# A scan kernel with experts: half a quad more of the products with C on GpSimdE, the last states copied there, and two groups of experts' products per slot

## The chip, the cores and the metric

One core of a Trainium2 chip runs the whole program. Time is device time of one launch in microseconds; the number that counts is the median of the runs shown. The profile is of one further execution, with its own time.

In the profile PE is TensorE's matmul, PEld its weight load, DVE is VectorE, ACT is ScalarE, POOL is GpSimdE, SP is SyncE, which here issues most DMAs.

## The reference, cut to what matters

The input x has 2 batches of 256 channels and 4096 positions (64 x 64). All is fp32.

```
# layer 0: group norm, then one selective scan with 256 inner channels
x = x + scan_block(gn(x), L0)
# layer 1, tokens t: norm, two selective scans with 512 inner channels, forward (f) and backward (b)
t = tokens(x)
xn = ln(ln(t)) * gamma + beta
t = t + scan_block(xn, f) + flip(scan_block(flip(xn), b)) + ln(t)
# experts: 8 of them, all used, weighted by a softmax over the mean of the batches
h = relu(bn(ln(t) @ W1[e] + b1)); h = relu(bn(h @ W2[e] + b2)); y = h @ Wo[e] + bo
t = t + sum_e w[e] * y[e]

def scan_block(x):
    xs, z = split(x @ W_in); xc = silu(conv4(xs)); dt, B, C = split(xc @ W_x); dt = softplus(dt @ W_dt + b)
    for each position:                                   # 16 states n for each inner channel d
        h[d, n] = h[d, n] * exp(dt[d] * A[d, n]) + dt[d] * xc[d] * B[n]
        y[d] = sum_n h[d, n] * C[n] + D[d] * xc[d]
    return (y * silu(z)) @ W_out
```

## The kernel before

**Stages.** After a short start (group norm of batch 0) come the scans: six jobs in this order, layer 0, f, b of batch 0, then of batch 1. A job runs over 8 chunks of 512 positions. Then comes the experts' stage, for what is left of the 8 experts on 8 chunks of 2 batches (128 units).

**Quads and passes.** 128 inner channels times 16 states are laid on the partitions so that one tile of 128 x 4 x 512 (a quad, tile `bq`) holds four groups of 32 channels by four states. Eight quads (two blocks j of 128 channels, four groups of states sg each) are a pass. Layer 0 has one pass per chunk, f and b have two: 80 passes, 640 quads. A quad is scanned in two halves of 128 x 1024; a half quad is a slot, the unit of the hand-written order, 16 to a pass.

**One quad's way.** POOL multiplies dt*x by B into `bq` (`emit_b`, L652, 128x2048), three quads ahead of the scan. ACT computes the decay exp(dt*A) of a half into a PSUM tile `da` (`emit_decay`, L662; two buffers) and joins the state carried from the chunk before (L673). DVE scans the half (`emit_scan`, L683). Then the product with C: for quads 0, 2 and 5 of a pass (`POOL_C`, L61) the scan writes back into `bq` and POOL multiplies the whole quad (`emit_times_c_quad`, L708); for the five others the scan writes into `da`, and DVE multiplies each half out of `da` into `bq` (`emit_times_c`, L692). PE sums over the states (`emit_sum`, L713, 128*32 weights `stack`) into `y`; DVE gates y (L732). The last state of each quad goes into `h_state` for the next chunk (`emit_carry`): ACT copies it from `da` (L702, two columns per half) or from `bq` (L704, four columns per quad), and for the POOL quads the product may overwrite `bq` only after that copy.

**Order.** Every engine works in the order in which the program issues to it; the loop at L1002 writes this order out, slot by slot. Within a slot: SP's loads, PE's work (`pe`, the sums, `pe2`), ACT's carry and next decay and `act`, then DVE: queue `dve0`, the scan, queue `dve`, the product with C; then POOL by the table `POOL_AT` (L64; "c0" is the product of quad 0, "b3" the B product three quads on), and queue `pool`. The `Slots` object holds work placed at a slot and queue.

**Work beside the scans.** While a chunk is scanned, the next one is prepared (`prepare`): in-projection xs and z (L412), convolution (L450), x-projection (L479), dt (L499), softplus, the gate z: PE at a slot, ACT's tanh (L537) one slot later, DVE's L541 into `sz` two slots later in queue `dve0`, ahead of that slot's scan. For f and b the slots of dt and z lie in the second pass of the chunk before, as do POOL's products xdt (L515) and f's norm (`norm`, L377 to L398: DVE divides, POOL adds, ACT applies the affine map at L385, one slot after the division). When b has finished a chunk, its features are normalised (`features`) and the experts can begin on it.

**The experts' planner** (`experts`, L837 to L894) fills PE's spare time in the scans. It walks the slots and keeps sums of what each slot already holds (`sl.count`: products, ACT operations, PSUM banks with the slots for which they are held). PE may take `PE_ROOM` 3.8 products a slot and be `PE_BEHIND` 2.5 behind; ACT likewise. One expert on one chunk of one batch is three layers (W1, W2, Wo) of two groups m of two matmuls; `follows` says the earliest slot of a layer's next group. At most one group is put into a slot. The units so placed are written to DRAM; 67 of the 128 are done before the scans end, the eight chunks of batch 0 and 3 experts of chunk 7 of batch 1.

**The experts' stage** (from L1050) does the 61 left: for each, W1 and W2 on PE (L1189) with ACT's relu (L1193), weights on DVE (L1200), Wo on PE (L1208). Chunks with something left are in `rest`, those complete in both batches in `whole` (none before). Side work is placed between: the routing of the next chunk (`routes`), the bias and the weighted sums of units done early (`sums`; L1159 and L1160 on DVE).

Of the kernel before, what the change touches and what calls it, by code (L numbers as in the profile page):

```python
# [44 lines left out]
ALU = mybir.AluOpType  # L45
AX = mybir.AxisListType

P = 128
NB, C, L = 2, 256, 4096
KC = C // P  # L50
# [9 lines left out]

POOL_C = (0, 2, 5)  # L61

SUMS = {(0, 0): (-1,), (2, 0): (0, 1), (4, 0): (2, 3), (5, 1): (4,), (7, 0): (5, 6)}
POOL_AT = {0: "b3", 1: "c0 b4", 2: "b5", 3: "c2 b6", 4: "b7", 5: "b8", 6: "c5 b9", 7: "b10"}  # L64
HUGE = 1e37


# [62 lines left out]
def hybrid_kernel(ctx: ExitStack, tc: tile.TileContext, a: dict, out: bass.AP):  # L130
# [53 lines left out]
    with ExitStack() as st:  # L184
# [129 lines left out]
        def norm(i):  # L314
# [79 lines left out]
            for d, queue, fn in (  # L394
                (-48, "sp", load_x), (-44, "pe", mean), (-43, "dve", centre), (-42, "act", square),
                (-41, "pe", variance), (-40, "act", roots), (-39, "dve", divide), (-39, "pool", add),
                (-38, "act", affine), (-36, "sp", store),
            ):  # L398

                sl.put(s0 + d + (6 if c == 0 else 0), queue, fn)  # L400
# [2 lines left out]
            sl.count(s0 - 43, 0, 1)  # L403
            sl.count(s0 - 41, 2, 4, (2,))
            sl.count(s0 - 40, 0, 0, (1,))
            sl.count(s0 - 39, 0, 2)

        def in_proj(job, ck, half, j, name):
            ps = psp.tile([P, T], F32, tag="ps", name=name)
# [8 lines left out]
        def prepare(i):  # L418
# [109 lines left out]
            def gate(j):  # L528

                v = {}  # L530

                def pe():
                    v["ps"] = in_proj(job, ck, 1, j, f"z_{tag}_{j}")

                def act():
                    v["th"] = wk.tile([P, T], F32, tag="th", name=f"thz_{tag}_{j}", bufs=3)
                    nc.scalar.activation(v["th"], v["ps"], AF.Tanh, scale=0.5)  # L537

                def dve():
                    ck["sz", j] = wk.tile([P, T], F32, tag="sz", name=f"sz_{tag}_{j}", bufs=8)  # L540
                    nc.vector.scalar_tensor_tensor(  # L541
                        ck["sz", j], v["th"], 1.0, v["ps"], ALU.add, ALU.mult
                    )

                return (0, "pe", pe), (1, "act", act), (2, "dve0", dve)

            def put(slot, work):
                for d, queue, fn in work:
# [5 lines left out]
            for j in range(nj):  # L554
                put(at["xs"][j], xs(j))
                sl.count(s0 + at["xs"][j], 2, 1, (1,))
                put(at["dt"][j], softplus(j))
                sl.count(s0 + at["dt"][j], 1, 3, (2,))
                sl.count(s0 + at["z"][j], 2, 1, (1,))
            for jp in range(nj // 2):  # L560
                put(at["conv"][jp], conv(jp))
                sl.count(s0 + at["conv"][jp], 5, 1, (1, 2))
# [82 lines left out]
        def over_groups(t):  # L645
            return t.rearrange("p (o t) -> p o t", o=1).to_broadcast([P, SG, T])
# [20 lines left out]
        def emit_join(g, h):  # L667
# [4 lines left out]
            if c:  # L672
# [2 lines left out]
                    scale=cks[i]["a0", j][:, h, sg : sg + 1], bias=bq[g][:, q, 0:1],  # L675
                )

        def emit_scan(g, h):
            i, j, sg = at(g)
            job, c = steps[i]  # L680
            d = da[g, h].rearrange("p q t -> p (q t)")
            b = bq[g][:, 2 * h : 2 * h + 2, :].rearrange("p q t -> p (q t)")
            nc.vector.tensor_tensor_scan(  # L683
                b if quads[g][2] in POOL_C else d, d, b,
                job.h[:, j, sg, 2 * h : 2 * h + 1] if c else 0.0, ALU.mult, ALU.add,
            )

# [9 lines left out]
        def emit_carry(g, h):  # L697

            i, j, sg = at(g)
            d, two = da.pop((g, h)), slice(2 * h, 2 * h + 2)  # L700
            if quads[g][2] not in POOL_C:
                nc.scalar.copy(steps[i][0].h[:, j, sg, two], d[:, :, T - 1])  # L702
            elif h:
                nc.scalar.copy(steps[i][0].h[:, j, sg, :], bq[g][:, :, T - 1])  # L704

        def emit_times_c_quad(g):
            i, j, sg = at(g)
            nc.gpsimd.tensor_tensor(bq[g], bq[g], over_groups(cks[i]["bc", 1, sg]), ALU.mult)  # L708

        def emit_sum(g):  # L710
            i, j, sg = at(g)
# [125 lines left out]
        def experts():  # L837
# [4 lines left out]
            def fits(slot):  # L842

                at = sum(b[0] <= slot for b in banks)
                both = banks[:at] + [(slot, slot + 1, 0)] + banks[at:]
                return all(
                    both[k - 3][1] + both[k][2] <= both[k][0] for k in range(max(3, at - 2), min(len(both), at + 4))
                    if at in range(k - 3, k + 1)
                )
# [9 lines left out]
            def follows(l):  # L859

                k, m = divmod(len(times[l]), KC)
                if k == len(todo):
                    return None
                waits = [(l - 1, k * KC + 1, 2)] if l else []
                if m:
                    waits.append((l, k * KC, 1))
                elif k:

                    waits.append((l, k * KC - 1, 6 if l == 0 and todo[k][-1] == 0 else 5))
                    if l < 2:  # L870
                        waits.append((l + 1, k * KC - 1, 0))
                if any(n >= len(times[w]) for w, n, _ in waits):
                    return None
                return max([todo[k][0] + 3] + [times[w][n] + d for w, n, d in waits])

            for slot in range(last):
                behind = max(0.0, behind) + sl.products.get(slot, 0) + sums_in(slot) - PE_ROOM
                act_behind = max(0.0, act_behind) + sl.acts.get(slot + 1, 0) - ACT_ROOM
                if behind + 2 > PE_BEHIND or act_behind + 1.3 > ACT_BEHIND or not fits(slot):
                    continue  # L880
                for l in (2, 1, 0):
                    at = follows(l)
                    if at is None or slot < at:
                        continue
                    banks.insert(sum(b[0] <= slot for b in banks), (slot, slot + 1, 0))
                    times[l].append(slot)
                    behind += 2
                    act_behind += 1 if l == 2 else 1.3
                    break
            put = [  # L890
                (*item[1:], [times[l][k * KC + m] for l in range(3) for m in range(KC)])
                for k, item in enumerate(todo) if (k + 1) * KC <= len(times[2])
# [109 lines left out]
        for g in range(nq):  # L1002
            i, jp, n = quads[g]
            for h in range(2):
# [24 lines left out]
                sl.run(slot, "dve0")  # L1029
                emit_scan(g, h)  # L1030
                sl.run(slot, "dve")
                if n not in POOL_C:
                    emit_times_c(g, h)

                if h == 0:
                    for what in POOL_AT.get(n, "").split():
                        m = g - n + int(what[1:])
                        if what[0] == "c":
                            emit_times_c_quad(m)
                        else:  # L1040
                            want_b(m)
                sl.run(slot, "pool")
# [7 lines left out]
    with ExitStack() as st:  # L1050
# [171 lines left out]
        side = {i: [] for i in rest}  # L1222
        for at, i in enumerate(rest):
            after = rest[at + 1 : at + 2]
            now = sums(i)
            if at:
                for j in whole[at - 1 : at]:
                    now += sums(j)
            ahead = []
            for j in whole[at : at + 1] + after:  # L1230
                ahead += routes(j)
            every = max(1, len(now) // max(1, len(ahead)))
            work = side[i]
            while now or ahead:
                work += ahead[:1] + now[:every]
                ahead, now = ahead[1:], now[every:]
# [143 lines left out]
```

## Time and profile before

| what | us |
|---|---|
| median of 3 runs | 5331.44 (5330.82 to 5335.3) |
| the profiled execution | 5329.55 |
| its span | 5327.7 |
| DVE busy in it | 4647.7 |
| PE busy in it | 4401.2 |
| POOL busy in it | 4271.5 |
| ACT busy in it | 3707.4 |
| first scan starts | 61.1 |
| last scan starts | 4588.9 |

The busy times are over the whole span, which mixes the two stages; the page's row of 40 slices shows DVE and POOL full for the first 34 of them and PE full in the last five. A row of a group reads: line, engine, operation, output from inputs, shape, count, then busy time and the mean of one. A row of waits reads: who waited for whom, total us, times, longest.

### The profile page before, as it was taken

What the parts mean: (1) busy time and instruction counts of PE and PEld (TensorE: products, weight loads), DVE (VectorE), ACT (ScalarE), POOL (GpSimd) and SP (SyncE); (2) the same over time, 40 slices, a digit from 0 to 9 for tenths busy, and PEclk for the clock granted to TensorE, in tenths of its full rate; (3) what the DMA queues carried; (4) which work ended last, traced back from release to release, by engine and by line L of the source; (5) the groups of instructions that cost most, each with busy time, mean ns of one, the idle gap of its engine ahead of it and who ended that gap; (6) DMA issues with size and microseconds to landing.
All of it is one profiled execution on the core that took longest, in us unless ns stands there. A gap on an engine that the chain in (4) does not pass through costs nothing.

```text
span 5327.7 us, 47305 instructions
## 1 busy us (share of the span) xinstructions
PE 4401.2 (83%) x14920; PEld 1499.7 (28%) x14920; DVE 4647.7 (87%) x3117; ACT 3707.4 (70%) x7728; POOL 4271.5 (80%) x1118
## 2 busy tenths in 40 slices
PE   5677767766678898888878888888998988699999
PEld 1122222221122233222222232233332332244444
DVE  6999999999999999999989999999999999554333
ACT  5677676776767777878887777788778877422332
POOL 6898999999998999998989999999999999411010
PEclk8778788888889999999999999899999999899999
DMA  4445433344334554455555444454545444332332
GB/s 172 139 173 180 139 124 134 127 152 147 131 129 156 189 177 160 164 175 181 191 192 178 160 157 155 166 186 163 178 149 184 171 167 159 132 138 103 111 103 75
DMA packets 306860, 821.11 MB, mean 154 GB/s; under 512 B 34664, under 2 KB 96112, under 8 KB 264624
## 3 DMA queue, kind: packets, MB, share of 16 engines
q1 hardware_dynamic: 302896, 792.78, 43.5%
q0 software_dynamic: 3712, 25.30, 1.2%
q8 instruction: 118, 1.93, 0.1%
q14 instruction: 134, 1.10, 0.1%
HBM read 637.48 MB, written 180.49 MB: 154 GB/s over the span
## 4 chain that ended last, share of the span: by engine, by line
DVE 42%; PE 26%; ACT 12%; issue 9%; POOL 5%; DMA 3%; SPq 0%; DVEq 0%; POOLq 0%; ACTq 0%
DVE da L683 21%; DVE bq L692 8%; PE hp L1189 8%; DVE bq L683 8%; ACT da L662 5%; PE y L1208 4%; PE e L903 3%; POOL bq L652 3%; PE y L713 2%; PE conv L450 2%; PE xs L412 2%; PE o L751 2%; DMA rdt<-dtd 1%; DVE sz L541 1%; PE dbc L479 1%
## 5 line engine op out<-in xcount | busy, mean ns | idle before, releaser
L652 POOL TENSOR_TENSOR bq<-rxdt,bc 128x2048 f32<-128x2048 f32 x640 | 2891.9, 4542 | 42.6 <-issue 20.5
L662 ACT ACTIVATE da<-rdt,w_a 128x512 f32<-128x512 f32 x2560 | 1756.4, 686 | 90.2 <-DVE bq L683 43.9
L683 DVE TENSOR_TENSOR_SCAN da<-da,h_state,bq 128x1024 f32<-128x1024 f32 x700 | 1643.9, 2348 | 12.7 <-issue 8.0
L708 POOL TENSOR_TENSOR bq<-bq,bc 128x2048 f32<-128x2048 f32 x240 | 1086.5, 4527 | 300.9 <-ACT h_state L704 279.8
L713 PE MATMUL y<-bq,stack 128*32 128x512 f32 x5120 | 849.7, 678 | 340.0 <-POOL bq L708 207.1
L692 DVE TENSOR_TENSOR bq<-da,bc 128x1024 f32<-128x1024 f32 x800 | 978.4, 1223 | 24.0
L683 DVE TENSOR_TENSOR_SCAN bq<-da,h_state,bq 128x1024 f32<-128x1024 f32 x420 | 965.1, 2334 | 24.2 <-ACT da L662 24.2
L702 ACT COPY h_state<-da 128x2 f32<-128x2 f32 x799 | 125.8, 157 | 794.0 <-DVE bq L692 792.7
L903 PE MATMUL e<-eh,ew 128*128 128x512 f32 x1072 | 539.6, 631 | 55.4 <-ACT eh L914 27.5
L1193 ACT ACTIVATE h<-hp,of,sc 128x512 f32<-128x512 f32 x244 | 189.6, 777 | 391.6 <-PE hp L1189 375.0
L673 ACT ACTIVATE bq<-h_state,bq,a 128x1 f32<-128x1 f32 x1120 | 431.9, 386 | 0.0
L713 PEld LDWEIGHTS y<-bq,stack 128*32 128x32 f32 x5120 | 152.3, 117 | 984.9 <-issue 376.8
L412 PE MATMUL z<-nx,w_in 128*128 128x512 f32 x640 | 337.9, 656 | 69.5 <-DVE sp L511 46.8
L412 PE MATMUL xs<-nx,w_in 128*128 128x512 f32 x640 | 338.2, 663 | 39.4 <-DVE xc L464 30.3
L450 PE MATMUL conv<-xs,w_conv 64*64 64x512 f32 x2560 | 329.6, 623 | 6.5 <-DVE sp L511 3.6
L903 PEld LDWEIGHTS e<-eh,ew 128*128 128x128 f32 x1072 | 196.2, 197 | 398.4 <-issue 231.8
L751 PE MATMUL o<-sz,w_out 128*128 128x512 f32 x640 | 299.7, 608 | 0.0
L903 PE MATMUL e<-en,ew 128*128 128x512 f32 x536 | 261.3, 614 | 26.5 <-DVE fcen L799 13.3
L1200 DVE TENSOR_TENSOR h<-h,wb 128x1024 f32<-128x1024 f32 x61 | 74.3, 1221 | 210.5 <-ACT h L1193 192.4
L1132 POOL DMA_DIRECT2D w_dram<-wts x8 | 4.3, 544 | 315.3 <-ACT wts L1130 315.3
L720 PE MATMUL y<-xc,w_d 128*128 128x512 f32 x320 | 186.6, 667 | 71.3 <-DVE sz L732 71.3
L515 POOL TENSOR_TENSOR xdt<-sp,xc 128x512 f32<-128x512 f32 x160 | 203.2, 1274 | 44.3 <-DVE sp L511 44.3
(138 smaller groups left out, 5446.2 us busy)
## 6 DMA issues: line engine op xcount, KB each, us to landing
rxdt<-xdtd SPq DMA_DIRECT2D x160, 1024.0 KB, 6.3
rdt<-dtd SPq DMA_DIRECT2D x160, 1024.0 KB, 5.9
bc<-bcd SPq DMA_DIRECT2D x384, 256.0 KB, 3.1
dtd<-sp SPq DMA_DIRECT2D x160, 256.0 KB, 3.6
xdtd<-xdt SPq DMA_DIRECT2D x160, 256.0 KB, 2.8
ew<-in_W SPq DMA_DIRECT2D x134, 256.0 KB, 4.1
u<-eu SPq DMA_DIRECT2D x67, 512.0 KB, 3.9
u<-u SPq DMA_DIRECT2D x67, 512.0 KB, 3.6
```

The costliest lines, as they stand in the source:

```text
L412: nc.tensor.matmul(ps, job.w["in", half][:, k, j * P : (j + 1) * P], rhs, start=(k == 0), stop=(k == KC - 1),)
L450: nc.tensor.matmul(v[r][64 * col : 64 * col + 64, :], job.w["conv"][rows, 2 * jp + j, k, :], ck["xs", jp][rows, j, k : k + T] if k < 4 els ...
L652: nc.gpsimd.tensor_tensor(bq[g], ck["rxdt", j], over_groups(ck["bc", 0, sg]), ALU.mult)
L662: nc.scalar.activation(da[g, h][:, k, :], cks[i]["rdt", j][:, q, :], AF.Exp, scale=steps[i][0].w["a"][:, j, q * SG + sg : q * SG + sg + 1],)
L673: nc.scalar.activation(bq[g][:, q, 0:1], job.h[:, j, sg, q : q + 1], AF.Identity, scale=cks[i]["a0", j][:, h, sg : sg + 1], bias=bq[g][:, ...
L683: nc.vector.tensor_tensor_scan(b if quads[g][2] in POOL_C else d, d, b, job.h[:, j, sg, 2 * h : 2 * h + 1] if c else 0.0, ALU.mult, ALU.add,)
L692: nc.vector.tensor_tensor(bq[g][:, two, :], d, cks[i]["bc", 1, sg].rearrange("p (o t) -> p o t", o=1).to_broadcast([P, 2, T]), ALU.mult,)
L708: nc.gpsimd.tensor_tensor(bq[g], bq[g], over_groups(cks[i]["bc", 1, sg]), ALU.mult)
L713: nc.tensor.matmul(y[i, j][q * CG : (q + 1) * CG, :], stack, bq[g][:, q, :], start=False, stop=(sg == SG - 1),)
L751: nc.tensor.matmul(v[m], job.w["out"][:, j, m * P : (m + 1) * P], ck["sz", j], start=False, stop=(j == job.nj - 1),)
L903: nc.tensor.matmul(ps, ew[l][:, k, m * P : (m + 1) * P], key[x][:, k, :], start=(k == 0), stop=(k == KC - 1),)
L1189: nc.tensor.matmul(ps, we[f"W{l + 1}", e][:, k, m * P : (m + 1) * P], x[:, k, :], start=(k == 0), stop=(k == KC - 1),)
```

## The change

1. In every second pass (`g // QN % 2`; for f and b the second pass of a chunk) the first half of quad 4 joins the POOL quads: its scan writes into `bq` and POOL multiplies 128x1024 by C (`h4` ahead of `b8`).
2. POOL copies the last states of all its quads itself, just before the product ("tensor_copy" ahead of "tensor_tensor"), in place of ACT.
3. The gate's DVE operation moves from queue `dve0` to `dve`, that is from ahead of the scan to behind it, and the planner counts its bank for two slots. The norm's affine map moves one slot later (except in a job's first chunk).
4. The planner may put more than one group into a slot, both groups of a layer into the same one, and the planner's count of the norm's affine moves by one slot.
5. In the experts' stage the sums of a complete chunk come first in a chunk's side work, and no longer between the routings.

```diff
--- before.py
+++ after.py
@@ -60,8 +60,10 @@
 
 POOL_C = (0, 2, 5)
 
+POOL_HALF = (4, 0)
+
 SUMS = {(0, 0): (-1,), (2, 0): (0, 1), (4, 0): (2, 3), (5, 1): (4,), (7, 0): (5, 6)}
-POOL_AT = {0: "b3", 1: "c0 b4", 2: "b5", 3: "c2 b6", 4: "b7", 5: "b8", 6: "c5 b9", 7: "b10"}
+POOL_AT = {0: "b3", 1: "c0 b4", 2: "b5", 3: "c2 b6", 4: "b7", 5: "h4 b8", 6: "c5 b9", 7: "b10"}
 HUGE = 1e37
 
 
@@ -394,7 +396,7 @@
             for d, queue, fn in (
                 (-48, "sp", load_x), (-44, "pe", mean), (-43, "dve", centre), (-42, "act", square),
                 (-41, "pe", variance), (-40, "act", roots), (-39, "dve", divide), (-39, "pool", add),
-                (-38, "act", affine), (-36, "sp", store),
+                (-37 if c else -38, "act", affine), (-36, "sp", store),
             ):
 
                 sl.put(s0 + d + (6 if c == 0 else 0), queue, fn)
@@ -403,7 +405,7 @@
             sl.count(s0 - 43, 0, 1)
             sl.count(s0 - 41, 2, 4, (2,))
             sl.count(s0 - 40, 0, 0, (1,))
-            sl.count(s0 - 39, 0, 2)
+            sl.count(s0 - 38, 0, 2)
 
         def in_proj(job, ck, half, j, name):
             ps = psp.tile([P, T], F32, tag="ps", name=name)
@@ -542,7 +544,7 @@
                         ck["sz", j], v["th"], 1.0, v["ps"], ALU.add, ALU.mult
                     )
 
-                return (0, "pe", pe), (1, "act", act), (2, "dve0", dve)
+                return (0, "pe", pe), (1, "act", act), (2, "dve", dve)
 
             def put(slot, work):
                 for d, queue, fn in work:
@@ -556,7 +558,7 @@
                 sl.count(s0 + at["xs"][j], 2, 1, (1,))
                 put(at["dt"][j], softplus(j))
                 sl.count(s0 + at["dt"][j], 1, 3, (2,))
-                sl.count(s0 + at["z"][j], 2, 1, (1,))
+                sl.count(s0 + at["z"][j], 2, 1, (2,))
             for jp in range(nj // 2):
                 put(at["conv"][jp], conv(jp))
                 sl.count(s0 + at["conv"][jp], 5, 1, (1, 2))
@@ -675,13 +677,18 @@
                     scale=cks[i]["a0", j][:, h, sg : sg + 1], bias=bq[g][:, q, 0:1],
                 )
 
+        def on_pool(g, h):
+
+            n = quads[g][2]
+            return n in POOL_C or (n, h) == POOL_HALF and g // QN % 2
+
         def emit_scan(g, h):
             i, j, sg = at(g)
             job, c = steps[i]
             d = da[g, h].rearrange("p q t -> p (q t)")
             b = bq[g][:, 2 * h : 2 * h + 2, :].rearrange("p q t -> p (q t)")
             nc.vector.tensor_tensor_scan(
-                b if quads[g][2] in POOL_C else d, d, b,
+                b if on_pool(g, h) else d, d, b,
                 job.h[:, j, sg, 2 * h : 2 * h + 1] if c else 0.0, ALU.mult, ALU.add,
             )
 
@@ -698,14 +705,17 @@
 
             i, j, sg = at(g)
             d, two = da.pop((g, h)), slice(2 * h, 2 * h + 2)
-            if quads[g][2] not in POOL_C:
+            if not on_pool(g, h):
                 nc.scalar.copy(steps[i][0].h[:, j, sg, two], d[:, :, T - 1])
-            elif h:
-                nc.scalar.copy(steps[i][0].h[:, j, sg, :], bq[g][:, :, T - 1])
-
-        def emit_times_c_quad(g):
+
+        def emit_times_c_quad(g, groups=SG):
             i, j, sg = at(g)
-            nc.gpsimd.tensor_tensor(bq[g], bq[g], over_groups(cks[i]["bc", 1, sg]), ALU.mult)
+            b = bq[g][:, :groups, :]
+            nc.gpsimd.tensor_copy(steps[i][0].h[:, j, sg, :groups], b[:, :, T - 1])
+            nc.gpsimd.tensor_tensor(
+                b, b,
+                cks[i]["bc", 1, sg].rearrange("p (o t) -> p o t", o=1).to_broadcast([P, groups, T]), ALU.mult,
+            )
 
         def emit_sum(g):
             i, j, sg = at(g)
@@ -863,7 +873,7 @@
                     return None
                 waits = [(l - 1, k * KC + 1, 2)] if l else []
                 if m:
-                    waits.append((l, k * KC, 1))
+                    waits.append((l, k * KC, 0))
                 elif k:
 
                     waits.append((l, k * KC - 1, 6 if l == 0 and todo[k][-1] == 0 else 5))
@@ -876,17 +886,16 @@
             for slot in range(last):
                 behind = max(0.0, behind) + sl.products.get(slot, 0) + sums_in(slot) - PE_ROOM
                 act_behind = max(0.0, act_behind) + sl.acts.get(slot + 1, 0) - ACT_ROOM
-                if behind + 2 > PE_BEHIND or act_behind + 1.3 > ACT_BEHIND or not fits(slot):
-                    continue
-                for l in (2, 1, 0):
+                for l in (2, 1, 1, 0, 0):
                     at = follows(l)
                     if at is None or slot < at:
                         continue
+                    if behind + 2 > PE_BEHIND or act_behind + 1.3 > ACT_BEHIND or not fits(slot):
+                        break
                     banks.insert(sum(b[0] <= slot for b in banks), (slot, slot + 1, 0))
                     times[l].append(slot)
                     behind += 2
                     act_behind += 1 if l == 2 else 1.3
-                    break
             put = [
                 (*item[1:], [times[l][k * KC + m] for l in range(3) for m in range(KC)])
                 for k, item in enumerate(todo) if (k + 1) * KC <= len(times[2])
@@ -1029,7 +1038,7 @@
                 sl.run(slot, "dve0")
                 emit_scan(g, h)
                 sl.run(slot, "dve")
-                if n not in POOL_C:
+                if not on_pool(g, h):
                     emit_times_c(g, h)
 
                 if h == 0:
@@ -1037,6 +1046,9 @@
                         m = g - n + int(what[1:])
                         if what[0] == "c":
                             emit_times_c_quad(m)
+                        elif what[0] == "h":
+                            if on_pool(m, 0):
+                                emit_times_c_quad(m, SG // 2)
                         else:
                             want_b(m)
                 sl.run(slot, "pool")
@@ -1222,15 +1234,14 @@
         side = {i: [] for i in rest}
         for at, i in enumerate(rest):
             after = rest[at + 1 : at + 2]
-            now = sums(i)
+            now, work = sums(i), side[i]
             if at:
                 for j in whole[at - 1 : at]:
-                    now += sums(j)
+                    work += sums(j)
             ahead = []
             for j in whole[at : at + 1] + after:
                 ahead += routes(j)
             every = max(1, len(now) // max(1, len(ahead)))
-            work = side[i]
             while now or ahead:
                 work += ahead[:1] + now[:every]
                 ahead, now = ahead[1:], now[every:]
```

## The prediction

> **What bounds the kernel now.** I read the page first, then a table of busy time by stretch, then who waits for whom, then the order of time. The kernel has two stages. The scans (the 80 passes of 16 half quads) fill 61.07 to 4592.4 us; the six stretches below are the jobs (layer 0, f, b of each batch) and the seventh is the experts' stage, 735.3 us.
>
> ```profile
> core 0: us, PE busy (x) PEld busy (x) DVE busy (x) ACT busy (x) POOL busy (x), PEclk, DMA share, GB/s
> 61.07:540.70 479.63, 335.61 (x1166) 97.05 (x1168) 453.02 (x287) 352.81 (x746) 432.94 (x111) 0.80 0.48 163
> 540.70:1438.80 898.10, 632.35 (x2316) 184.19 (x2312) 868.21 (x565) 642.03 (x1398) 839.49 (x214) 0.85 0.40 137
> 1438.80:2341.20 902.40, 756.68 (x2712) 250.21 (x2708) 872.62 (x578) 689.04 (x1474) 831.73 (x208) 0.92 0.47 160
> 2341.20:2815.20 474.00, 398.98 (x1418) 129.59 (x1420) 438.21 (x286) 390.22 (x807) 423.37 (x109) 0.96 0.57 191
> 2815.20:3716.30 901.10, 781.39 (x2794) 263.83 (x2792) 868.88 (x564) 711.86 (x1518) 842.55 (x215) 0.93 0.49 166
> 3716.30:4592.40 876.10, 763.63 (x2716) 260.26 (x2712) 857.13 (x547) 686.55 (x1459) 812.68 (x201) 0.95 0.47 158
> 4592.40:5327.70 735.30, 701.14 (x1688) 302.16 (x1688) 271.95 (x255) 211.27 (x283) 79.88 (x56) 0.98 0.33 115
> ```
>
> In the scans DVE is busy 4358 of 4531 us (96%), POOL 4183 (92%). So DVE bounds this stage and POOL stands 175 us behind it: work that leaves DVE for POOL is worth only what POOL can take. In the experts' stage PE is busy 95%.
>
> Inside a chunk the two passes differ. Here are passes 52 and 53 (job f) and 72 and 73 (job b):
>
> ```profile
> 3040.70:3093.00 52.30, 49.58 (x210) 16.89 (x207) 51.96 (x34) 39.83 (x89) 48.44 (x12) 1.00 0.43 144
> 3093.00:3154.40 61.40, 47.86 (x141) 16.03 (x141) 57.66 (x40) 50.03 (x104) 57.72 (x17) 0.86 0.54 189
> 4156.40:4208.70 52.30, 51.03 (x214) 17.54 (x211) 51.95 (x34) 40.82 (x91) 48.87 (x12) 1.00 0.35 121
> 4208.70:4267.30 58.60, 49.67 (x151) 16.39 (x150) 56.55 (x40) 48.38 (x102) 55.41 (x16) 0.91 0.60 202
> ```
>
> The second pass of a chunk is the long one, and in job f DVE stands still 3.7 us of it. The waits say why:
>
> ```profile
> DVE sz L541 <- ACT thz L537: 66.3, 39, 4.1
> DVE xc L464 <- ACT thx L459: 34.6, 14, 15.3
> DVE bq L683 <- ACT da L662: 28.1, 24, 2.2
> POOL bq L708 <- ACT h_state L704: 279.8, 113, 7.2
> ```
>
> The gate's L541 stands ahead of the scan and waits for ACT's tanh: 66 us. Most of POOL's rest is the product with C (L708) waiting until ACT has copied the last states.
>
> **What the Trainium skill says.** "GPSIMD Engine Reference", 3.1 "Elementwise — side-by-side cycle accounting", gives 4497 ns for a two-input operation of 2048 columns. The trace agrees: 4542 and 4527 ns, starts 4.48 us apart. The same page, 1 "Specifications", says the SBUF interfaces are shared with VectorE, contended by DVE instructions with two SBUF inputs; L683 and L692 take one input from PSUM, and no run here shows such a collision. "Perfetto Trace Analysis", "GPSIMD Engine Instruction", advises timing by spacing of starts, which I do. "TensorE: Matmul & The Clock Gate", Part 1, says idleness throttles PE: granted clock rises here from 0.80 to 0.96 as PE's busy share in the jobs rises from 0.70 to 0.84, so products that fill gaps partly pay for themselves.
>
> **The change part by part.**
>
> 1. *Half quad 4 in every second pass.* 40 passes, one L692 each. Spacing of starts gives what a half quad costs DVE:
>
> ```profile
> 3049.31 2.35 DVE L683 TENSOR_TENSOR_SCAN da<-da,h_state,bq 128x1024 f32<-128x1024 f32 x1
> 3051.70 1.23 DVE L692 TENSOR_TENSOR bq<-da,bc 128x1024 f32<-128x1024 f32 x1
> 3052.84 4.58 DVE L683 TENSOR_TENSOR_SCAN bq<-da,h_state,bq 128x1024 f32<-128x1024 f32 x2
> 3057.34 2.33 DVE L683 TENSOR_TENSOR_SCAN da<-da,h_state,bq 128x1024 f32<-128x1024 f32 x1
> ```
>
> With product 3052.84 - 3049.31 = 3.53 us; without, (3057.34 - 3052.84)/2 = 2.25. So DVE loses 1.28 x 40 = 51 us. POOL gains 40 products of 128x1024 at 2.30 us (spacing behind L381, same shape: 3018.18 to 3020.48), 92 us.
>
> 2. *POOL copies last states.* 240 + 40 = 280 copies of 4 or 2 columns, and each product waits for POOL's own copy. The trace shows none. Below: spacings of 1.23 us for 512 columns and 4.48 for 2048 leave 0.15 us at no columns. Above: nothing so small is near 1 us; POOL's setup rows of 128x128 take 0.20 and 0.29 us; I bound it at 0.7 us, four times the lower, for the wait on its own result. A gain is not excluded: the link over ACT goes (in a waiting case, scan end 3045.29, ACT's copy to 3045.53, product 3045.60), about 0.2 us in the 113 waiting products. I take 0.3 us each: 84 us. Queued behind a waiting copy are its product and the B products of quads three ahead; DVE's scans need them only six half quads later, PE's sums at once. ACT loses 240 copies of 190 ns and 40 of 157 (52 us); ACT is busy 77% of the scans, so this costs and gives nothing by itself.
>
> 3. *Gate behind the scan* (dve0 to dve). L541 gets 2.3 us more; the mean wait was 66.3/39 = 1.7 us, the longest 4.1. Alone worth some 50 to 60 us, if nothing else is late next. The later affine (one slot) relieves ACT, which waited 16 us for POOL's L381. Its price is a PSUM bank held a slot longer; the planner counts it.
>
> What is late next is POOL, so I add up a pair of passes (one chunk of f or b, two of layer 0), means over the jobs:
> - f: 112.4 us now, DVE 108.6, POOL 105.1. After: DVE 107.3, POOL 105.1 + 2.3 + 7 x 0.3 = 109.5. POOL is now the fuller; with 1 us of waits 110.5. Gain 1.9 x 16 = 30 us.
> - b: 111.2 now, DVE 108.1, POOL 102.8. After: DVE 106.8, POOL 107.2; with 2 us of waits (3 now) 109.1. Gain 2.1 x 16 = 34.
> - layer 0: 119.2 now, after 1.3 less for the product and 1.2 for the gate (9.9 us of that wait lie in its 8 pairs). Gain 2.5 x 8 = 20.
> Together 84 us.
>
> 4. *Two products in one slot.* Counted in the program's order: 888 expert matmuls before the end of the scans instead of 804, so 74 experts instead of 67; 54 are left. In the last stage one expert takes PE
>
> ```profile
> 5252.04 4.29 PE hp L1189 x10
> 5256.33 0.01 issue
> 5256.34 2.84 PE hp L1189 x6
> 5259.19 3.43 PE y L1208 x8
> 5262.62 4.29 PE hp L1189 x10
> ```
>
> 10.58 us, on the chain that ends the program. 7 x 10.58 = 74 us less. Chunk 7 is then complete in both batches; its routing and its 16 weighted sums stay in the stage, beside PE (DVE 37% busy there; 7 more sums at 1.32 + 1.40 = 2.7 us are 19 us). Changed order of that side work: nothing, hidden by the same idle DVE; uncovered, at most the 16 us standstill at the stage's start (4642.74, "issue", on the chain) could grow or vanish, so 74 +- 10. In the scans PE takes on 84 matmuls at (539.6 + 261.3)/804 = 1.0 us, 84 us or 1.6 per pass over 53 passes, and SP 28 more DMAs (21 weights, 7 stores) that wait in order behind PE. The fullest even passes of b already carry 18 matmuls at 52.3 us, as long as those with 14, and the new order gives 18 nearly everywhere. Not free everywhere: from 0 to 40 us through later y, conv and z; I take 15. The new short slots want the decay sooner: 28.1 us over 240 such quads is 0.12 each; 40 x 0.12 = 5.
>
> Sum: scans -84 + 15 + 5 = -64, experts' stage -74, together -138. The profiled execution took 5329.6 us, its span 5327.7 and 1.9 around it: 5329.6 - 138 = 5191.6. The median of the runs is 1.9 higher: 5193.5, and I say 5193.
>
> **The rivals.**
> - *POOL becomes the bound outright.* A copy with its wait costs 0.7 us: f needs 105.1 + 2.3 + 4.9 = 112.3, all of today's 112.4; b 110.0 plus 1 of wait, nothing; layer 0 keeps some 10. Scans -10, stage -74: 5247. For it: the profile has no row for the copy, and pass 53 already fills POOL 57.7 of 61.4 us. Against: spacing leaves little fixed cost.
> - *DVE gets everything.* POOL's lag in the second pass is made good in the first (48.4 of 52.3), the lead of three quads (21 us) hides it, and the ACT link's removal pays for the copies. DVE's 51 + 55 of the gate, less 10: scans -96, stage -76: 5159. For it: the lead; against: f's sum of 109.5 allows only -46 in f.
> - *Slower.* One mechanism, the copy on POOL (L708's place, before each product). With 92 + 280c on top of 4183 and about 60 us of waits, POOL fills 4531 + 74 us, that is eats the gain of the experts' stage, at c = 0.97 us. At c = 1.3 the scans take 4699, 168 more, less 74: 5425.
> - *PE too full.* The two products in a slot delay y and z by more than my 15, 60 us: 5238. For it: PE 50 of 52 us busy in first passes; against: the rising clock.
> That the change doesn't do what it says is excluded by the order of the program: 40 halves, 280 copies and 74 experts stand in it.
>
> **How the numbers follow.** Forecast 0.60 (its own range 5170 to 5222: stage +-10, copies 0.15 to 0.5 us, PE 0 to 30), POOL outright 0.12, DVE everything 0.15, PE too full 0.07, slower 0.06. The range leaves out the slower case and the far halves of the others: 5152 to 5245. 0.2% is 11 us, about what a measurement of this kernel tells from no change. Faster by more: 0.92; within: 0.02 (the far end of PE too full); slower: 0.06.
>
> **What would show it right or wrong.** Stage after the last scan: near 661 us, 54 x 24 products. Scans: about 4467 us. POOL's copies: spacing to their product near 0.3 us. L541's wait for thz: under 20 us. Pairs of f: near 110.5 with POOL over 98% busy and L708's wait small; if DVE is instead the fuller, the second rival holds. POOL busy over 99% with DVE waiting for L652 shows the first. I am wrong if the copies cost over 0.7 us, or if DVE's waits for y (L732), thx or thz grow by over 40 us.

## The result and the profile after

The changed kernel takes 5211.78 us (median of 4 runs, 5208.79 to 5213.06), the kernel before 5332.59 us beside it: ratio 0.9773, 95% interval 0.976 to 0.9787. That is 121 us less; 138 were forecast, and the range from 5170 to 5222 us holds. The profiled execution took 5213.1 us, its span is 5211.3.

The same cut of the span as before, behind the last scan and its product: start, end and length of the stretch, busy us (instructions) of each engine, granted clock, DMA share, GB/s. First the kernel after, then the one before, cut in two likewise.

```profile
60.71:4529.40 4468.69, 3633.04 (x13280) 1201.78 (x13280) 4286.82 (x2781) 3468.84 (x7160) 4323.39 (x1373) 0.91 0.47 164
4529.40:5211.30 681.90, 634.21 (x1520) 274.20 (x1520) 280.28 (x261) 189.29 (x255) 78.92 (x56) 0.97 0.36 129
```

```profile
61.07:4592.40 4531.33, 3668.65 (x13112) 1185.13 (x13112) 4358.08 (x2821) 3472.51 (x7398) 4182.75 (x1053) 0.90 0.47 160
4592.40:5327.70 735.30, 701.14 (x1688) 302.16 (x1688) 271.95 (x255) 211.27 (x283) 79.88 (x56) 0.98 0.33 115
```

The scans are 62.6 us shorter (64 forecast), the experts' stage 53.4 (74 forecast). The order of the two fullest engines in the scans has turned: POOL is busy 96.7%, DVE 95.9%. PE does 168 more instructions in the scans and is busy 36 us less there; over the whole program the sums into y (L713, now L723) are busy 779.4 us instead of 849.7. Why they are is not shown. In the experts' stage PE is busy 66.9 us less and idle 13.5 us more (47.7 of 681.9 us, before 34.2 of 735.3).

Pairs of passes of the jobs f and b in the changed kernel, cut at a pass's first scan (passes 52, 53, 72, 73 again):

```profile
3001.70:3054.60 52.90, 49.05 (x214) 17.34 (x213) 52.55 (x34) 40.89 (x89) 52.66 (x15) 1.00 0.42 150
3054.60:3111.10 56.50, 45.68 (x138) 15.56 (x137) 55.71 (x39) 48.43 (x96) 56.06 (x22) 0.88 0.54 188
4096.80:4150.10 53.30, 51.44 (x221) 17.93 (x220) 52.64 (x35) 41.03 (x90) 53.06 (x16) 1.00 0.41 144
4150.10:4206.30 56.20, 48.57 (x146) 17.24 (x145) 54.38 (x37) 48.20 (x96) 54.42 (x20) 0.91 0.61 206
```

In this pair of f POOL works 108.72 of 109.4 us. The second pass has shrunk from 61.4 to 56.5 us, the first has grown from 52.3 to 52.9.

Means over all pairs of a job, worked out from the same cuts at every pass:

| pair of passes | before | after | DVE, POOL busy after | forecast |
|---|---|---|---|---|
| f (16) | 112.4 | 109.5 | 107.1, 108.7 | 110.5 |
| b (16) | 111.2 | 110.1 | 106.7, 107.0 | 109.1 |
| layer 0 (8) | 119.2 | 119.4 | 108.2, 109.2 | 116.7 |

The waits that answer to those shown of before (who waited for whom, total us, times, longest):

```profile
DVE sz L742 <- PE y L723: 43.4, 36, 4.7
DVE bq L690 <- ACT da L664: 36.0, 28, 2.4
DVE da L690 <- ACT da L664: 28.8, 42, 1.4
DVE xc L466 <- ACT thx L461: 15.4, 12, 4.7
...
POOL h_state L714 <- DVE bq L690: 73.0, 43, 5.0
```

The gate's wait for the tanh is gone (2.4 us for L543). The wait for y, which L742 gates, has come up from 12.8 to 45.4 us over the whole program: PE itself now waits 337 us for POOL's product (L715), where it waited 207.

The copies, in the order of time on POOL in pass 53 (start, duration):

```profile
3093.91 0.19 POOL L714 COPY h_state<-bq 128x2 f32<-128x2 f32 x1
3094.18 2.35 POOL L715 TENSOR_TENSOR bq<-bq,bc 128x1024 f32<-128x1024 f32 x1
3096.48 4.54 POOL L654 TENSOR_TENSOR bq<-rxdt,bc 128x2048 f32<-128x2048 f32 x1
3100.97 0.19 POOL L714 COPY h_state<-bq 128x4 f32<-128x4 f32 x1
3101.24 4.54 POOL L715 TENSOR_TENSOR bq<-bq,bc 128x2048 f32<-128x2048 f32 x1
```

From the copy's start to its product's it is 0.27 us (the median of all 280 too), 0.3 was taken. The half product takes 2.30 us of POOL, as forecast.

### The profile page after: what moved, and what is told of

It reads as the page before. It is cut to its first block, busy times and chain, and to the rows that moved or that the text cites. A ratio compares the mean times of both kernels' runs of the same rounds, so it can differ in the third digit from the quotient of the medians.

```text
span 5211.3 us, 47295 instructions
## 1 busy us (share of the span) xinstructions
PE 4298.0 (82%) x14920; PEld 1488.2 (29%) x14920; DVE 4584.8 (88%) x3083; ACT 3681.8 (71%) x7462; POOL 4410.2 (85%) x1438
## 5 line engine op out<-in xcount | busy, mean ns | idle before, releaser
L690 DVE TENSOR_TENSOR_SCAN da<-da,h_state,bq 128x1024 f32<-128x1024 f32 x664 | 1559.5, 2349 | 38.7 <-ACT da L664 27.3
L715 POOL TENSOR_TENSOR bq<-bq,bc 128x2048 f32<-128x2048 f32 (+1 forms) x280 | 1179.6, 4213 | 22.5
L723 PE MATMUL y<-bq,stack 128*32 128x512 f32 x5120 | 779.4, 687 | 362.1 <-POOL bq L715 337.2
L690 DVE TENSOR_TENSOR_SCAN bq<-da,h_state,bq 128x1024 f32<-128x1024 f32 x456 | 1052.3, 2337 | 27.9 <-ACT da L664 27.8
L699 DVE TENSOR_TENSOR bq<-da,bc 128x1024 f32<-128x1024 f32 x760 | 928.2, 1221 | 18.7
L912 PE MATMUL e<-eh,ew 128*128 128x512 f32 x1184 | 582.4, 621 | 60.5 <-DVE sp L513 20.5
L723 PEld LDWEIGHTS y<-bq,stack 128*32 128x32 f32 x5120 | 144.9, 118 | 935.1 <-POOL bq L715 458.6
L1205 ACT ACTIVATE h<-hp,of,sc 128x512 f32<-128x512 f32 x216 | 167.7, 777 | 345.0 <-PE hp L1201 328.5
L912 PE MATMUL e<-en,ew 128*128 128x512 f32 x592 | 290.5, 622 | 47.3 <-DVE fcen L809 21.5
L923 ACT ACTIVATE eh<-e,of,sc 128x512 f32<-128x512 f32 x296 | 223.7, 769 | 37.9 <-PE e L912 36.7
L501 PE MATMUL dt<-dbc,w_dt 64*128 64x512 f32 x320 | 197.2, 701 | 44.5 <-ACT dbc L488 27.7
```

The lines of the kernel that those rows point to most:

```text
L690: nc.vector.tensor_tensor_scan(b if on_pool(g, h) else d, d, b, job.h[:, j, sg, 2 * h : 2 * h + 1] if c else 0.0, ALU.mult, ALU.add,)
L699: nc.vector.tensor_tensor(bq[g][:, two, :], d, cks[i]["bc", 1, sg].rearrange("p (o t) -> p o t", o=1).to_broadcast([P, 2, T]), ALU.mult,)
L715: nc.gpsimd.tensor_tensor(b, b, cks[i]["bc", 1, sg].rearrange("p (o t) -> p o t", o=1).to_broadcast([P, groups, T]), ALU.mult,)
L723: nc.tensor.matmul(y[i, j][q * CG : (q + 1) * CG, :], stack, bq[g][:, q, :], start=False, stop=(sg == SG - 1),)
L912: nc.tensor.matmul(ps, ew[l][:, k, m * P : (m + 1) * P], key[x][:, k, :], start=(k == 0), stop=(k == KC - 1),)
```

## The experiments

Each ran three rounds beside the kernel before, whose medians were 5330.9 to 5333.4 us. "Scans" and "stage" are cut from the one profile of each, and so are the means of a pair of passes. How far such cuts scatter can be seen where the code of a stretch is the same: in the changed kernel, e4, e8 and e12 the scans take 4461 to 4469 us, a pair of f 109.4 to 109.5, of b 110.1 to 110.2, of layer 0 118.6 to 119.4; in the changed kernel and in e1, e2, e3, e6, e7, e9 and e10 the stage takes 679 to 685 us.

**e1: without the half quad.**

```diff
-            return n in POOL_C or (n, h) == POOL_HALF and g // QN % 2
+            return n in POOL_C
```

> The changed kernel without its half quad: quad 4 stays whole with VectorE, 40 products and 40 copies leave GpSimdE (40 x 2.57 = 103 us), 51 us come back to VectorE. Theory one (GpSimdE is now the fuller engine in the jobs f, and its lateness makes VectorE wait for y): the half is worth far less than 51 us, some 20 to 30: 5232 to 5242. Theory two (VectorE still bounds everywhere): the whole 51 us come back, 5263. A third (the late products cost more than the half saves): 5212 or less.

Measured 5227.8 us (ratio 0.9806, 0.9791 to 0.9821): the half is worth 16 us, not DVE's 51. In f a pair takes 109.7 us without it and 109.5 with it: DVE's 108.2 us of work fall to 107.1, POOL's 106.4 rise to 108.7, and the pair is hardly shorter. In b it is 111.1 against 110.1; in layer 0 118.7, inside the scatter. DVE's wait for y is 24.3 us without the half and 43.4 with it. That is theory one, with a gain under its lower end.

**e2: last states copied by ACT again.**

```diff
+            elif quads[g][2] not in POOL_C:
+                nc.scalar.copy(steps[i][0].h[:, j, sg, two], bq[g][:, two, T - 1])
+            elif h:
+                nc.scalar.copy(steps[i][0].h[:, j, sg, :], bq[g][:, :, T - 1])
...
-            nc.gpsimd.tensor_copy(steps[i][0].h[:, j, sg, :groups], b[:, :, T - 1])
```

> The changed kernel with the last states of the GpSimdE quads copied by ScalarE, as before, the half quad too: 280 x 0.27 = 76 us leave GpSimdE, the product waits for ScalarE again. Theory one (GpSimdE bounds the jobs f): a pair of passes of f loses up to 1.9 us until VectorE bounds it, 10 to 25 us in all: 5187 to 5202. Theory two (the link over ScalarE was what cost): 113 waits x 0.2 us come back and VectorE bounds anyway, 5212 to 5235.

Measured 5224.2 us (0.9797, 0.978 to 0.9813): 12 us more, although 76 us of work left POOL. I had the sign wrong. POOL's products wait 158 us for ACT's copies (63 times), where the copies on POOL wait 73 us for the scan. So the number is theory two's, but the 12 us do not lie in these many waits: a pair of f takes 109.8 us and one of b 110.0, nearly as with copies on POOL. The scans are 13.7 us longer, and 13.3 of this is one pass, the second of layer 0 (75.5 us instead of 62.2). A small operation of DVE in it, which prepares the experts' scales once in the program, lasts 18 us. First DVE, then POOL, in this run:

```profile
137.59 18.13 DVE L840 TENSOR_TENSOR sc<-sc,bn 128x32 f32<-128x32 f32 x1
139.82 2.50 POOL L517 TENSOR_TENSOR xdt<-sp,xc 128x512 f32<-128x512 f32 x2
142.27 4.50 POOL L718 TENSOR_TENSOR bq<-bq,bc 128x2048 f32<-128x2048 f32 x1
146.72 8.95 POOL L654 TENSOR_TENSOR bq<-rxdt,bc 128x2048 f32<-128x2048 f32 x2
```

And in the changed kernel:

```profile
137.48 2.87 DVE L837 TENSOR_TENSOR sc<-sc,bn 128x32 f32<-128x32 f32 x1
131.25 9.05 POOL L654 TENSOR_TENSOR bq<-rxdt,bc 128x2048 f32<-128x2048 f32 x2
140.24 2.50 POOL L517 TENSOR_TENSOR xdt<-sp,xc 128x512 f32<-128x512 f32 x2
142.67 0.20 POOL L714 COPY h_state<-bq 128x4 f32<-128x4 f32 x1
```

In every profile this operation ends 0.04 to 0.05 us after one of POOL's ends. With the copies on ACT (before, e2, e6, e9) it is the sixth, 18.1 us on, and the pass takes 73 to 76 us; with the copies on POOL, in all the others, it is the first, after 2.8 to 2.9 us, and the pass takes 59 to 62. DVE reads both inputs from SBUF here, where the scans and the products with C take one from PSUM. That POOL's work holds it off fits these times; no run tried it alone, and why it gets in at the first end in one case and not in the other stays open.

**e3: the gate ahead of the scan again.**

```diff
-                return (0, "pe", pe), (1, "act", act), (2, "dve", dve)
+                return (0, "pe", pe), (1, "act", act), (2, "dve0", dve)
```

> The changed kernel with the gate's VectorE operation ahead of the scan again; the planner still counts its bank for two slots, so the experts' order is the same. Theory one (GpSimdE bounds f, where more than half of the 66 us of that wait lay): the wait returns to the profile, but GpSimdE hides much of it, 10 to 30 us: 5222 to 5242. Theory two: all of it comes back, 5270.

Measured 5213.5 us (0.9779, 0.9764 to 0.9793): no difference from 5211.8, less than either theory. The waits traded places. In this kernel's scans:

```profile
DVE sz L543 <- ACT thz L539: 48.0, 44, 5.4
DVE bq L690 <- ACT da L664: 35.3, 27, 4.3
DVE sz L742 <- PE y L723: 18.0, 23, 3.1
DVE nx L379 <- ACT r L180: 7.4, 15, 1.7
DVE da L690 <- ACT da L664: 7.1, 18, 1.5
```

48 us for the tanh came, and 25 us for y and 22 for the decay went. A wait of 66 us in the table of before was thus no promise of 66 us. (Without the half the same edit is worth 27 us: e7.)

**e4: the side work of the experts' stage as before.** The complete chunk's sums are again mixed with the chunk's own:

```diff
-            now, work = sums(i), side[i]
+            now = sums(i)
...
-                    work += sums(j)
+                    now += sums(j)
...
+            work = side[i]
```

> The changed kernel with the side work of the experts' stage in the order of before (a complete chunk's sums mixed with the chunk's own, between the routings). The stage took 682 us where 74 less than 735, 661, were expected. Theory one: the 20 us are lost because the 16 sums of chunk 7 stand first, with their loads in SP's queue; the old order brings back 10 to 20 us, 5192 to 5202. Theory two: the loss comes with a complete chunk in whatever order (its routing is squeezed into the first, shorter chunk): 5207 to 5217.

Measured 5216.0 us (0.9781, 0.9766 to 0.9795), stage 685.5: nothing comes back, as theory two has it. The changed order is worth nothing that can be told from scatter, as the prediction said, and is not what the stage lacks.

**e5: the planner of before** (one group per slot, its old counts), the rest as changed.

```diff
-            sl.count(s0 - 38, 0, 2)
+            sl.count(s0 - 39, 0, 2)
...
-                sl.count(s0 + at["z"][j], 2, 1, (2,))
+                sl.count(s0 + at["z"][j], 2, 1, (1,))
...
-                    waits.append((l, k * KC, 0))
+                    waits.append((l, k * KC, 1))
...
-                for l in (2, 1, 1, 0, 0):
+                if behind + 2 > PE_BEHIND or act_behind + 1.3 > ACT_BEHIND or not fits(slot):
+                    continue
+                for l in (2, 1, 0):
...
+                    break
```

> The changed kernel with the planner of before: one group per slot, its old counts, so 67 experts in the scans and 61 after them; half quad, copies and gate stay as changed. The stage should go back to 735 us. Theory one (the seven further experts cost the scans little, and the scans' gain comes from half, copies and gate): scans 4455 to 4470, in all 5250 to 5268. Theory two (a part of the scans' 63 us comes from the planner's new order, with PE fuller and its clock higher): scans above 4475, 5272 or more.

Measured 5263.2 us (0.9874, 0.9859 to 0.9889): scans 4468.3, with seven experts less the same as 4468.7; stage 735.9. That is theory one. In the changed scans PE's 84 further matmuls cost nothing that stands out: by the medians e5 is 51 us slower and by the profiles its stage is 54 us longer, which would leave them 3 us.

**e6: the planner alone.** The kernel before with the new planner and the new side order: no half, ACT's copies, gate ahead, affine at its old slot.

> The kernel before with the new planner and the new side order alone: no half quad, last states copied by ScalarE, gate ahead of the scan, the affine map at its old slot. 74 experts in the scans, stage near 682. Theory one (half, copies and gate cover for one another: undone one at a time they cost 16, 12 and 2 us, undone together all the 63): scans 4525 to 4545, 5268 to 5288. Theory two (they add up, 30 us, and the rest came from the planner): scans near 4500, 5242.

Measured 5298.1 us (0.9938, 0.9921 to 0.9954): scans 4553.4, stage 682.8. Here the same further experts cost 22 us of scans (DVE's wait for the tanh 80.6 us instead of 63.9). All else together is then worth 86 us, while undone one at a time half, copies and gate cost 16, 12 and 2: above theory one's range. But e6 also puts back the affine, which e9 prices at 42. Half, copies and gate alone are then worth 44 us together, against 30 undone one at a time.

**e7: copies and later affine, without half and gate.** e1's and e3's edits together.

> The changed kernel without the half quad and with the gate ahead of the scan: of the scans' edits the copies on GpSimdE and the later affine stay. Theory one (half and gate cover for one another in the jobs f: with neither, VectorE waits for the tanh again and GpSimdE has room): 5250 to 5265. Theory two (they add up: 16 and 2): 5228 to 5232.

Measured 5254.8 us (0.9858, 0.9843 to 0.9873). With e1, e3 and the changed kernel this makes a square, the copies, the affine and the planner being alike in all four:

| | gate ahead of the scan | gate behind it |
|---|---|---|
| quad 4 with DVE | 5254.8 | 5227.8 |
| half of it on POOL | 5213.5 | 5211.8 |

The half alone is worth 41 us, the gate alone 27, both 43. They do stand for one another: theory one. The pairs of passes show where:

| a pair of | neither | gate behind | half on POOL | both |
|---|---|---|---|---|
| f | 110.6 | 109.7 | 109.8 | 109.5 |
| b | 112.0 | 111.1 | 110.8 | 110.1 |
| layer 0 | 118.1 | 118.7 | 117.2 | 118.6 to 119.4 |

In f either does nearly all that both do, in b they nearly add up, and in layer 0 the gate behind the scan takes away what the half gives.

**e8: the complete chunk's sums divided.** Those of batch 1 go one chunk later.

```diff
-                    work += sums(j)
+                    late = sums(j)
+                    work += late[: 3 + E]
+                    side[after[0]] += late[3 + E :]
```

> The changed kernel with the weighted sums of the complete chunk 7 divided: those of batch 0 in the next chunk's side work as now, those of batch 1 one chunk later, so that no chunk has more than 16 or 17 sums. Theory one (24 sums in one chunk fill VectorE and SP's queue between 4640 and 4740 us, and PE stands 9 us): 5200 to 5207. Theory two (the lost 20 us of the stage lie in its start and its clock): 5209 to 5215.

Measured 5200.1 us (0.9754, 0.9739 to 0.9768), stage 673.6 instead of 681.9 us, below the scatter: theory one.

**e9: the planner and the later affine.** e6 with one number changed.

```diff
-                (-38, "act", affine), (-36, "sp", store),
+                (-37 if c else -38, "act", affine), (-36, "sp", store),
```

> The kernel with the planner alone (5298) plus the norm's affine map one slot later, nothing else. In the jobs f ScalarE stood up to 1.2 us for GpSimdE's L381 just ahead of the tanh for which VectorE waits. With copies and the later affine together the scans were 46 us shorter. Theory one (the affine is half of that): 5272 to 5284. Theory two (the copies are nearly all of it): 5292 to 5299.

Measured 5255.9 us (0.9855, 0.984 to 0.987): this one slot is worth 42 us, more than either theory, and with e7 at 5254.8 the copies without half and gate add 1. (That 1 is a sum: layer 0's second pass falls from 73.1 to 60.0 us, as in e2, while a pair of b rises from 111.6 to 112.0 and the stage by 5.7 us, within its scatter.) The reason stands in the order of time of ACT, with the gate on DVE behind it, in pass 53 of the kernel before (start, duration, in brackets the idle time ahead and what ended it):

```profile
3131.46 1.28 ACT L567 ACT_TABLE_LOAD   x1
3134.27 1.52 ACT L385 ACTIVATE nx<-cen,lngb 128x512 f32<-128x512 f32 x2 [1.53 <-POOL x L381]
3135.69 0.37 ACT L673 ACTIVATE bq<-h_state,bq,a 128x1 f32<-128x1 f32 x1
3135.97 1.40 ACT L662 ACTIVATE da<-rdt,w_a 128x512 f32<-128x512 f32 x2
3137.30 0.58 ACT L537 ACTIVATE thz<-z 128x512 f32<-128x512 f32 x1
3137.91 0.69 DVE L541 SCALAR_TENSOR_TENSOR sz<-thz,z 128x512 f32<-128x512 f32 x1 [3.16 <-ACT thz L537]
```

ACT waits 1.53 us for POOL's sum (the affine overwrites what the sum reads) and then works 1.5 us on the affine, all ahead of the decay and the tanh for which DVE stands 3.16 us. One slot later the affine comes behind the tanh, and wait and work both leave its way. In the changed kernel:

```profile
3093.98 1.41 ACT L664 ACTIVATE da<-rdt,w_a 128x512 f32<-128x512 f32 x2
3095.32 0.58 ACT L539 ACTIVATE thz<-z 128x512 f32<-128x512 f32 x1
3095.80 1.51 ACT L387 ACTIVATE nx<-cen,lngb 128x512 f32<-128x512 f32 x2
```

From e6 to e9 DVE's wait for the tanh in the scans falls from 80.6 to 42.2 us, 38 us, and the scans from 4553.4 to 4512.6. ACT stood for POOL's sum 12 times in e6 (18.1 us), and 12 of the 16 pairs of f are 1.6 to 4.2 us shorter in e9; the mean falls from 112.8 to 110.7, that of b from 111.7 to 111.6. In e6 the planner counts the affine one slot later than it stands, but in the kernel before, where the two agree, a pair of f takes 112.4 us, so that is at most 0.4 of the 2.1.

**e10: the changed kernel with the affine at its old slot** (e9's edit backwards).

> The changed kernel with the affine map at its old slot, one after the division. Theory one: GpSimdE is later than before, so ScalarE stands longer for its sum and passes that on to decays: 5222 to 5240. Theory two (GpSimdE bounds f anyway, which hides what ScalarE loses): 5208 to 5217.

Measured 5222.4 us (0.979, 0.9773 to 0.9806): 11 us, at the lower edge of theory one. DVE's wait for decays (L690, into `da`) rises from 28.8 to 55.9 us. Theory one's reason does not hold, though: ACT stands 11.8 us for POOL's sum, not longer than in the kernel before (16.1). With half, copies and gate in place, three quarters of the 42 us are hidden.

**e11: e8, and the gate ahead of the scan in layer 0 alone.**

```diff
-                return (0, "pe", pe), (1, "act", act), (2, "dve", dve)
+                return (0, "pe", pe), (1, "act", act), (2, "dve" if nj == 4 else "dve0", dve)
```

> The version with divided sums (5200), and in layer 0 alone the gate ahead of the scan again; f and b keep it behind. With the gate ahead everywhere a pair of passes of layer 0 took 117.2 us instead of 119.4, f and b 0.3 and 0.7 more. Theory one (behind the scan the gate delays the product with C there, and so the sum and y): 8 pairs x 2.2 = 18 us less, 5180 to 5190. Theory two (the 2.2 us are scatter of that one profile): 5196 to 5203.

Measured 5186.6 us (0.9724, 0.971 to 0.9739), faster than both kernels and in theory one's range. A pair of layer 0 takes 117.2 us, in e8 118.6. In its passes (120 to 535 and 2300 to 2770 us) DVE's wait for y falls from 16.5 us in e8 to 3.5, and that for the tanh of the gate rises to 17.9; the waits for the tanh of the convolution (L466) fall from 10.0 to 1.6 us and those for decays into `da` from 5.8 to 0.4. So more than y gets through sooner. That the gate behind the scan is what delays product, sum and y fits this, but the chain itself was not traced.

**e12: e8, and the complete chunk's routing one chunk later,** its sums in the two chunks after.

```diff
-                    work += late[: 3 + E]
-                    side[after[0]] += late[3 + E :]
+                    side[rest[at + 1]] += late[: 3 + E]
+                    side[rest[at + 2]] += late[3 + E :]
...
-            for j in whole[at : at + 1] + after:
+            for j in (whole[at - 1 : at] if at else []) + after:
```

> The version with divided sums, and the routing of the complete chunk 7 one chunk later too, its sums in the two chunks after that. The stage took 673.6 us there, 661 were expected. Theory one (the second routing in the first chunk makes PE wait for its input, 8.5 us at L1115, and run at a lower clock after it): stage 662 to 667, 5188 to 5195. Theory two (the rest lies in the start): 5197 to 5203.

Measured 5193.4 us (0.9734, 0.9719 to 0.9748), stage 660.0 us: theory one. In the changed kernel PE stood in the first chunk for the second routing's input:

```profile
4619.08 3.60 PE L1220 MATMUL y<-h,Wo 128*128 128x512 f32 x8
4630.33 3.58 PE L1115 MATMUL lt<-wr,nm 128*128 128x8 f32 x16 [7.66 <-POOL nm L1108]
```

and its Wo products waited 14.5 us for the weighted h, which DVE makes between the sums (6.3 us in the kernel before). e8 brings the second down to 7.7 us; with this edit the first is gone too:

```profile
PE y L1220 <- DVE h L1212: 6.8, 1, 6.8
```

e11 and e12 were not run together.

## Why the prediction was right, and where its parts were not

Of the signs set beforehand, f's pairs (109.5 us with POOL over 99% busy), the copies' spacing and the gate's wait came as said; the stage did not (681.9 us, 661 said).

**The scans** came out at 62.6 us against 64, but as a sum of errors that cancel, which is luck: by the table of pairs f gained 46 us (30 forecast, before 20 us of costs were taken off), b 18 (34), and layer 0 lost 2 (20). Built up one edit at a time, from the runs:

| step | time | difference |
|---|---|---|
| before | 5330.9 | |
| + planner, side order (e6) | 5298.1 | -33: stage -52, scans +22 (profiles) |
| + affine one slot later (e9) | 5255.9 | -42 |
| + copies on POOL (e7) | 5254.8 | -1: a sum, see e9 |
| + gate behind the scan (e1) | 5227.8 | -27 |
| + half quad (after) | 5211.8 | -16 |

- *Half quad:* the step said DVE's 51 us would be cut to what POOL can take. It held: 16 us last in line, next to nothing in f, where POOL now works 108.7 of 109.5 us (109.5 of 110.5 forecast). In another order of edits the same half is worth 41 (e3 against e7).
- *Copies:* 0.27 us each against 0.3. The price was right. The gain from the link over ACT, which I put at 0.2 us in 113 products and then left out, cannot be seen: what the copies are worth last in line, 12 us (e2), is the one operation in layer 0's second pass, which the prediction did not have in view. It says that no run shows a collision of DVE's operations with two inputs from SBUF and POOL; this operation, 18.12 us in the profile of before (L827), fits one.
- *Gate:* "some 50 to 60 us" for the gate alone. It is 27 after the affine and 2 last in line; the affine, which I named in a half sentence as a relief of 16 us of ACT's waiting, carries 42. The mistake was to read 16 us as the affine's whole price: ahead of the tanh stood the wait and the affine's own 1.5 us, and DVE paid for both.
- *Layer 0:* 20 us forecast, none got. With the gate ahead of the scan a pair takes 117.2 us (e3), 2.0 less than before where 2.5 were forecast; the gate behind the scan takes this back, and e11 turns that round.
- *PE:* I took 15 us. It is 22 in the old scans (e6) and next to none in the changed ones (e5). That products which fill gaps partly pay for themselves through the clock shows little here: from the kernel before to e6 it goes from 0.90 to 0.91 in the scans, which are 22 us longer.

**The experts' stage** is the term that was mis-sized: 53.4 us instead of 74. The step was 10.58 us for each of 7 experts, with chunk 7's routing and 16 sums "beside PE" at no cost. The 10.58 us hold: with that side work moved out of the first two chunks (e12) the stage is 660.0 us, where 661 were forecast, and PE is busy 627.5 us in it, 73.6 less than before. The cover failed, since a complete chunk's routing falls into the first chunk of the stage, together with another one, and its sums into the next, and PE, which works its queue in order, waited for both. From e12 to the changed kernel PE's idle time in the stage is 15 us longer (47.7 against 32.4), and the same 1520 matmul records take 6.7 us more, at a granted clock of 0.97 against 0.98. I had put +-10 on this; it was 20.

**The rivals.** "DVE gets everything" did not come: POOL is the fuller engine in f, and the half on it brings next to nothing there. (That POOL's load alone bounds f is not shown; e2 takes load off it and f is no faster.) "POOL outright" and "slower" needed copies of 0.7 and 0.97 us; they take 0.27. "PE too full" by 60 us is excluded by e5 for the changed kernel.

## What to carry to other kernels

The price of a badly placed operation can be far more than the wait that stands beside it in the table: here a wait of 16 us had a price of 42, since the operation's own time and the work queued behind it stood in the way as well. So look at what comes next in the queue. Waits that stand in the same stretch can cover for one another, so undoing edits one at a time can undervalue them (half and gate: 16 and 2 us last in line, 43 together), and a table of waits can't be added up. It can also credit an edit with something that is not its mechanism: the copies' 12 us stand in one pass, which only a cut pass by pass shows. Work "beside" a full engine was free here only where that engine's own queue did not wait for it; moving it to later chunks was worth 18 us (e8 and e12).

## What the runs showed of the hardware that was not expected

A copy of 128x2 or 128x4 on POOL takes 0.19 us, and a product that waits for it starts 0.27 us after the copy's start. The same copy on ACT takes 0.19 us too (45.6 us for 240 before).

One operation of DVE, 128x32 with both inputs in SBUF, took 18.1 us beside POOL's products in four profiles and 2.8 to 2.9 us in ten, each time until one of POOL's operations ended (e2). DVE's scans and products with C, with one input in PSUM, run beside POOL at 96% each.

ACT's table load of 1.28 us was followed by the next operation at once in the changed kernel (3091.92 + 1.28, next start 3093.21).
